# The list schedule of layer 0: a group's operations up to the end of LSTM 0 rank with the group in front of it

## The chip, the cores and the metric

The kernel runs on one core of a Trainium2 chip. The core has five engines with an instruction queue each: PE (matrix products, with weight loads shown as PEld), DVE (vector), ACT (activations and copies), POOL (a second elementwise engine) and SP, which here only issues DMAs. The metric is the device time of the whole program in microseconds (us); lower is better.

## The reference

The input is x, 128 graphs of 64 nodes with 256 features, and one 64 x 64 adjacency matrix. Four layers follow each other, each of the form x = x + layer(relu(layernorm(x))). Only layer 0 is touched by the change:

```python
h = relu(adj @ (h @ Wg0 + bg0))            # twice, with Wg0 and Wg1, per graph
h = relu(adj @ (h @ Wg1 + bg1))
for p in 1..4:                             # four LSTMs of window p
    wins = h[:, :nw*p].reshape(B*nw, p, 256)
    h[:, p-1::p] = lstm_last(Wih[p-1], Whh[p-1], bias, wins)
x = x + h
```

The LSTM of window 1 (here called LSTM 0) has a single step from a zero state, so it needs only the gates i, g and o, no recurrent product, and it overwrites every node. LSTM 1, 2 and 3 have 2, 3 and 4 steps. Layers 1 to 3 are a graph convolution with attention and a feed-forward part, a graph attention layer, and a spectral layer that needs the eigenvectors of a 64 x 64 matrix. That eigendecomposition is computed in the kernel too.

## The kernel before

The 128 graphs are packed in pairs into 64 token tiles of 128 rows. Layer 0 works on groups of GT = 8 tiles, so it has NG = 8 groups; layers 1 to 3 work on 16 groups of HT = 4 tiles.

No instruction is issued where it is written. Every call on an engine goes to a recorder (`Plan.record`), and at the end a list scheduler (`Plan.schedule`, lines 227 to 326) sets the order on each engine from a table of estimated costs, picks the buffers from the pools, and `Plan.issue` emits the whole program; this is why line 344 is the line of every instruction in the profile. The scheduler repeats: for each engine, among the operations whose inputs are done and whose buffers can be had, take the one that can start now with the lowest rank; of the engines, take the one that starts first.

Four things set that choice:

- The window (line 968): while group g is the oldest unfinished one, only groups g and g + 1 of layer 0 may be scheduled. When the last operation of group g has been placed, group g + 2 is admitted. Loads of its input may go one group earlier. This moment is called a boundary below: at boundary k (1 to 7), group k - 1 ends with its transposes and its residual add, and group k + 1 begins with its layernorm statistics (for boundary 7 there is no such group). While group 7 is the oldest, groups of the later layers are admitted.
- The rank (line 328): for layer 0 it is the group's number, less `op.lead`, then `-op.lead`, then the place in the program. An operation recorded with lead 1 thus ranks with the group in front of it, and ahead of that group's own operations.
- The pools: 12 buffers `big` of 128 x 1024, 10 buffers `mids` of 128 x 512, 8 PSUM banks. A group that isn't the oldest must leave some free for the oldest (line 971).
- The eigendecomposition runs beside layer 0 as a group of its own (its tiles are in `arena`). It is a long chain of small DVE operations; it goes last on DVE and ACT and first on PE.

One group of layer 0 (`layer0`, from line 1309) is, in the order of the program:

1. The lead part: statistics of 8 tiles (`ln_stats`: 16 DVE operations, then four small POOL operations for each half of the tiles), 8 ACT operations for normalisation and relu, and for each half a product with adj (`mix`, 32 matmuls of 64 x 64), ACT copies, 8 matmuls with `Wg[0]`, a DVE maximum, a second `mix` and DVE adds; then 8 matmuls of 128 x 512 with `Wg[1]`, each pair followed by a DVE maximum and a POOL add into `hT`.
2. LSTM 0 (`lstm_step` with p = 0): 24 matmuls of 128 x 512 with `Wih[0]`, 12 ACT activations of gates and 4 of tanh, 8 DVE products. It reads and overwrites `hT`, and is the first to use the buffer `cs`.
3. LSTM 1: step 0 is `lstm_step`, 12 matmuls of 128 x 512 with `Wih[1]`. Step 1 is `lstm_fast`, which makes each gate from seven products (Strassen's form) on half-size blocks: 56 matmuls of 128 x 256 with `Wih[1]`, `Whh[1]` and sums of their blocks (`sums`). It needs differences of blocks of the inputs, made on POOL from `hT` and on DVE from `hs` (`pieces`, four operations each).
4. LSTM 2 (in the same manner, 128 x 336 and 128 x 168), and LSTM 3 (plain steps of 128 x 256).
5. The end: 16 transposes of `hT` by PE, four DVE adds into x, and two DMAs to the scratch tensor `put`.

The lines that the change touches are line 1311, which sets the lead to 1 before the statistics, and line 1352, which sets it to 0:

```python
g = min(max(op.group - op.lead, 0), self.ends)
if op.group < REST:
    return (g, -op.lead, op.index)
```

Of the kernel before, what the change touches and what calls it, by code (L numbers as in the profile page):

```python
# [932 lines left out]
def gnn_kernel(ctx: ExitStack, tc: tile.TileContext, a, out):  # L933
# [47 lines left out]
    plan = Plan(tc, {"PE": nc.tensor, "V": nc.vector, "ACT": nc.scalar, "G": nc.gpsimd, "SP": nc.sync}, pools, late, reserve, window, EIG, REST + NT // HT - 6, slack)  # L981
    PE, V, ACT, G, SP = (plan.proxy(e) for e in ("PE", "V", "ACT", "G", "SP"))

    def bank(name):
        return plan.value("bank")
# [179 lines left out]
    def mix(src, m, nt, nc=2):  # L1165

        ps = [bank("mix") for i in range(2)]
        with plan.burst():  # L1170
            for c in range(nc):
                for t in range(nt):
                    for i, r in ((0, 0), (0, 1), (1, 0), (1, 1)):
                        PE.matmul(ps[i][half(r), bat(c * nt + t)], src(t, c)[half(i), half(r)], m(t)[half(i), half(i)], start=True, stop=True)
        return [p[:, :nc * nt * N].rearrange("p (c t n) -> p c t n", c=nc, t=nt) for p in ps]
# [5 lines left out]
    def fm():  # L1181

        return plan.value("big")[:, :2 * HT * P].rearrange("p (c n) -> p c n", c=2)

    def mid():
        return plan.value("mid")

    def transposes(srcs):

        pt = bank("tr")  # L1190
        for i, s in enumerate(srcs):
            PE.transpose(pt[:, i * P:(i + 1) * P], s, ident)
        return pt

    def ln_stats(src, n=HT):

        s = plan.value("stat")
        st = s[:, :6 * n].rearrange("p (t k) -> p t k", k=6)
        mv = s[:, 6 * n:8 * n].rearrange("p (t k) -> p t k", k=2)
        rs = s[:, 8 * n:10 * n].rearrange("p (k t) -> p k t", k=2)  # L1200
        for t in range(n):
            V.bn_stats(st[:, t, :], src[:, t, :])
            V.bn_aggr(mv[:, t, :], st[:, t, :])
        G.tensor_scalar(rs[:, 0, :], mv[:, :, 1], 1e-5, None, op0=ALU.add)
        G.tensor_tensor(rs[:, 0, :], rs[:, 0, :], mhalf[:, :n], op=ALU.pow)
        G.tensor_tensor(rs[:, 1, :], mv[:, :, 0], rs[:, 0, :], op=ALU.mult)
        G.tensor_scalar(rs[:, 1, :], rs[:, 1, :], -1.0, None, op0=ALU.mult)
        return lambda t: rs[:, 0, t:t + 1], lambda t: rs[:, 1, t:t + 1]
# [4 lines left out]
    def lstm_step(p, s, xs, hs, cs, ncol, dsts):  # L1213

        res = {}
        for m in range(2):
            sg = {}
            for nm, q, fn in GATES:
                if s == 0 and nm == "f":
                    continue  # L1220
                col = (q if p > 0 or q == 0 else q - 1) * D + m * P
                ps = bank("gate")[:, :ncol]
                for c in range(2):
                    PE.matmul(ps, Wih[p][:, c, col:col + P], xs(c), start=c == 0, stop=s == 0 and c == 1)
                if s:
                    for c in range(2):
                        PE.matmul(ps, Whh[p][:, c, col:col + P], hs[:, c, :ncol], start=False, stop=c == 1)
                sg[nm] = mid()[:, :ncol]
                ACT.activation(sg[nm], ps, fn, bias=bl[:, p, q * 2 + m:q * 2 + m + 1])
            if s:  # L1230
                V.tensor_mul(sg["i"], sg["i"], sg["g"])
                V.tensor_mul(cs[:, m, :ncol], cs[:, m, :ncol], sg["f"])
                V.tensor_add(cs[:, m, :ncol], cs[:, m, :ncol], sg["i"])
            else:
                V.tensor_mul(cs[:, m, :ncol], sg["i"], sg["g"])
            ACT.activation(sg["g"], cs[:, m, :ncol], AF.Tanh)
            res[m] = (sg["o"], sg["g"])
        for m in range(2):
            o, th = res[m]
            dst = dsts(m)  # L1240
            if len(dst.shape) == 4:
                o, th = (t.rearrange("p (b w t) -> p b w t", b=2, t=GT) for t in (o, th))
            V.tensor_mul(dst, o, th)
# [65 lines left out]
    def layer0(fetched):  # L1309
        x = fetched()  # L1310
        plan.lead = 1
        nl = 2 if plan.group == 0 else HT
        norms = [ln_stats(x[t // HT][:, t % HT:t % HT + nl, :], nl) for t in range(0, GT, nl)]
        ayT = [fm() for hf in range(2)]
        for t0 in range(0, GT, nl):
            sc, bi = norms[t0 // nl]
            two = lambda t: t.rearrange("p (t f) -> p t f", t=2)
            h, ah, y = ([], [], [])
            for j in range(0, nl, 2):
                h.append(two(mid()))  # L1320
                for t in (j, j + 1):
                    ACT.activation(h[-1][:, t - j, :], x[(t0 + t) // HT][:, (t0 + t) % HT, :], AF.Relu, scale=sc(t), bias=bi(t))
            ps = mix(lambda t, c: h[t // 2][:, t % 2, tok(c)], lambda t: adjTb, nl)
            for j in range(0, nl, 2):
                ah.append(mid().rearrange("p (c t) -> p c t", c=2))
                for i in range(2):
                    ACT.copy(ah[-1].rearrange("p c (t b n) -> p c t b n", t=2, b=2)[:, :, :, i, :], ps[i][:, :, j:j + 2, :])
            for j in range(0, nl, 2):
                yp = bank("y")
                for t in range(2):  # L1330
                    for c in range(2):
                        PE.matmul(yp[:, t * D:(t + 1) * D], ah[j // 2][:, c, tok(t)], Wg[0][:, c, :], start=c == 0, stop=c == 1)
                y.append(two(mid()))
                V.tensor_tensor(y[-1], two(yp), vec(nB0, 2), op=ALU.max)
            ps = mix(lambda t, c: y[t // 2][:, t % 2, tok(c)], lambda t: adjTb, nl)
            part = ayT[t0 // HT][:, :, t0 % HT * P:(t0 % HT + nl) * P].rearrange("p c (t b n) -> p c t b n", t=nl, b=2)
            for i in range(2):
                for c in range(2):
                    V.tensor_tensor(part[:, c, :, i, :], ps[i][:, c], vec(C0T[:, c, half(i)], nl), op=ALU.add)

        hT = [plan.value("big")[:, :P * GT] for m in range(2)]
        for hf in range(2):
            ts = slice(hf * GT // 2, (hf + 1) * GT // 2)
            for m in range(2):
                ps = bank("hT")
                for c in range(2):
                    PE.matmul(ps, Wg[1][:, c, tok(m)], ayT[hf][:, c, :], start=c == 0, stop=c == 1)
                dst = hT[m].rearrange("p (n t) -> p n t", t=GT)[:, :, ts]
                b1 = [B1T[:, i, m, :].unsqueeze(2).to_broadcast([P, P, GT // 2]) for i in range(2)]
                V.tensor_tensor(dst, ps.rearrange("p (t n) -> p n t", n=P), b1[0], op=ALU.max)  # L1350
                G.tensor_tensor(dst, dst, b1[1], op=ALU.add)
        plan.lead = 0
        cs, hs = fm(), fm()
        for hf in range(2):
            cols = slice(hf * 512, (hf + 1) * 512)
            lstm_step(0, 0, lambda c: hT[c][:, cols], None, cs, 512, lambda c: hT[c][:, cols])
        for p in range(1, 4):
            k = p + 1
            nw = N // k
            if p == 3:  # L1360
                last = plan.ops[-1]
            for s in range(k):
                def win(c):
                    return hT[c].rearrange("p (b n t) -> p b n t", b=2, t=GT)[:, :, s:s + (nw - 1) * k + 1:k, :]
                ncol = 2 * GT * nw
                dst = win if s == p else lambda c: hs[:, c, :ncol]
                if s and p in (1, 2):
                    w = ncol // 2
                    lstm_fast(p, lambda c, n: win(c)[:, n], lambda c, n: hs[:, c, n * w:(n + 1) * w], cs, w, dst)
                else:  # L1370
                    lstm_step(p, s, win, hs, cs, ncol, dst)

        plan.behind = last
        x = fetched()
        plan.behind = None
        for t0 in range(0, GT, 2):
            pt = transposes([hT[c].rearrange("p (n t) -> p n t", t=GT)[:, :, t0 + t] for t in range(2) for c in range(2)])
            xt = flat(x[t0 // HT][:, t0 % HT:t0 % HT + 2, :])
            V.tensor_add(xt, xt, pt)
        return x  # L1380
# [293 lines left out]
```

## Time and profile before

| | us |
|---|---|
| median of 3 runs (2164.06 to 2165.33) | 2164.6 |
| the profiled execution: its own time | 2165.9 |
| the profiled execution: span from first to last instruction | 2164.1 |
| PE idle in the span (2164.1 less 2112.6 busy) | 51.5 |
| granted PE clock, mean | 0.996 |

The trace divides the span in four. Up to 50 us the first inputs and weights arrive. From there to about 1220 us the groups of layer 0 follow each other, one boundary about every 165 us. From boundary 7 at about 1220 us to 1370 us, group 7 is alone with the end of the eigendecomposition. From 1370 us on, layers 1 to 3 run. Idle time of PE is read from the table of windows (a window's length less PE's busy time), and its cause from the timeline, where the bracket behind an entry names the idle time ahead of it and the engine whose result ended it.

### The profile page before, as it was taken

The numbers are of one execution on the slowest core, as the hardware profiler recorded it, in microseconds if no ns is written. First come the engines' busy times: TensorE is split into PE (matmuls) and PEld (weight loads), VectorE is DVE, ScalarE is ACT, GpSimd is POOL, SyncE is SP. The second block draws the span as 40 slices with busy tenths as digits, with TensorE's granted clock in tenths as the row PEclk, the third lists the DMA queues.
The fourth block names the chain that finished last, engine by engine and source line by source line (L and its number), as shares of the span: only waits on it lengthen the run. The fifth ranks groups of instructions, "written<-read, shape, count | busy, mean of one in ns | idle before, by whom it ended". The sixth has DMA issues, their size and how long they took to land.

```text
span 2164.1 us, 45598 instructions
## 1 busy us (share of the span) xinstructions
PE 2112.6 (98%) x16580; PEld 1630.7 (75%) x16580; DVE 1800.3 (83%) x7402; ACT 1079.8 (50%) x2331; POOL 653.1 (30%) x968
## 2 busy tenths in 40 slices
PE   8999999999999999999999999999999999999997
PEld 6688688688678678678778688766777767776776
DVE  5888788889899999899989887568878868885797
ACT  3354354354354354345345345456566655645673
POOL 7221211210200110110110113654456745554353
PEclk9999999999999999999999999999999999999999
DMA  5000100100100100100000213000010000000001
GB/s 205 2 3 22 41 3 22 40 1 21 40 1 20 40 1 20 40 1 21 26 1 23 69 40 97 21 1 2 21 41 21 21 22 21 12 11 11 1 2 60
DMA packets 44866, 57.67 MB, mean 27 GB/s; under 512 B 8928, under 2 KB 38496, under 8 KB 44640
## 3 DMA queue, kind: packets, MB, share of 16 engines
q1 hardware_dynamic: 43536, 53.71, 7.6%
q8 instruction: 130, 2.13, 0.4%
q10 hardware_dynamic: 1104, 1.05, 0.2%
q14 instruction: 96, 0.79, 0.1%
HBM read 37.53 MB, written 16.78 MB: 25 GB/s over the span
## 4 chain that ended last, share of the span: by engine, by line
PE 83%; DVE 11%; POOL 2%; ACT 1%; DMA 1%; issue 1%; SPq 0%; DVEq 0%; ACTq 0%
PE bank L344 83%; DVE arena L344 3%; DVE big L344 3%; DVE stat L344 2%; DVE mids L344 1%; DVE sums L344 1%; POOL stat L344 1%; POOL sums L344 1%; DMA Wih<-in_WihT_dram 1%; ACT mids L344 0%; ACT arena L344 0%; DMA Whh<-in_L_b_dram 0%; DMA big<-put 0%; ACT big L344 0%; SPq L344 0%
## 5 line engine op out<-in xcount | busy, mean ns | idle before, releaser
L344 PE MATMUL bank<-big,Wih 128*128 128x256 f32 (+3 forms) x2400 | 748.2, 435 | 18.7 <-DVE arena L344 9.3
L344 PEld LDWEIGHTS bank<-big,Wih 128*128 128x128 f32 x2400 | 439.9, 190 | 205.0 <-issue 114.4
L344 ACT ACTIVATE mids<-bank,bl 128x256 f32<-128x256 f32 (+3 forms) x528 | 275.4, 528 | 407.3 <-PE bank L344 403.5
L344 PE MATMUL bank<-big,Whh 128*128 128x256 f32 (+2 forms) x1624 | 431.0, 368 | 3.5 <-DVE big L344 3.5
L344 DVE TENSOR_TENSOR arena<-arena 64x21 f32<-64x21 f32 (+5 forms) x2255 | 372.9, 196 | 35.8 <-POOL arena L344 8.2
L344 PEld LDWEIGHTS bank<-big,Whh 128*128 128x128 f32 x1624 | 294.3, 190 | 42.5 <-issue 10.1
L344 PE MATMUL bank<-big,sums 128*128 128x168 f32 (+2 forms) x1728 | 268.8, 307 | 0.0
L344 PEld LDWEIGHTS bank<-big,sums 128*128 128x128 f32 (+1 forms) x1728 | 225.4, 178 | 16.0 <-issue 3.9
L344 POOL TENSOR_SCALAR stat<-stat 128x4 f32<-128x4 f32 (+1 forms) x228 | 67.9, 299 | 485.4 <-DVE stat L344 472.5
L344 ACT COPY mids<-bank 128x168 f32<-128x168 f32 (+2 forms) x393 | 132.1, 357 | 138.1 <-PE bank L344 135.1
L344 DVE TENSOR_TENSOR big<-mids 128x512 f32<-128x512 f32 (+2 forms) x256 | 142.8, 565 | 31.3 <-ACT mids L344 28.6
L344 ACT ACTIVATE mids<-mids,bl 128x336 f32<-128x336 f32 (+2 forms) x192 | 102.4, 540 | 71.4 <-DVE mids L344 67.6
L344 DVE TENSOR_TENSOR mids<-bank,mids 128x168 f32<-128x168 f32 (+2 forms) x307 | 112.9, 372 | 25.8 <-PE bank L344 22.3
L344 DVE SCALAR_TENSOR_TENSOR arena<-arena 64x1 f32<-64x1 f32 (+15 forms) x565 | 120.9, 237 | 7.5 <-POOL arena L344 3.9
L344 POOL TENSOR_TENSOR big<-big 128x168 f32<-128x168 f32 (+1 forms) x24 | 16.8, 712 | 359.9 <-DVE arena L344 132.2
L344 POOL TENSOR_TENSOR stat<-stat,mhalf 128x4 f32<-128x4 f32 (+1 forms) x114 | 122.1, 1072 | 5.7
L344 ACT ACTIVATE mids<-big 128x256 f32<-128x256 f32 (+2 forms) x176 | 89.4, 509 | 67.7 <-DVE big L344 48.8
L344 PE MATMUL bank<-Wih,big 128*128 128x256 f32 (+1 forms) x512 | 111.7, 358 | 0.2 <-ACT big L344 0.2
L344 DVE TENSOR_SCALAR arena<-arena 64x1 f32<-64x1 f32 (+9 forms) x537 | 104.8, 202 | 8.4 <-POOL arena L344 0.8
L344 DVE TENSOR_TENSOR big<-big,mids 128x256 f32<-128x256 f32 (+2 forms) x200 | 99.3, 498 | 11.1 <-ACT mids L344 10.2
L344 PEld LDWEIGHTS bank<-Wih,big 128*128 128x128 f32 x512 | 87.7, 190 | 15.4 <-issue 4.5
L344 ACT COPY big<-bank 128x512 f32<-128x512 f32 x108 | 59.9, 587 | 55.9 <-PE bank L344 50.8
(357 smaller groups left out, 3568.0 us busy)
## 6 DMA issues: line engine op xcount, KB each, us to landing
big<-in_x_dram SPq DMA_DIRECT2D x30, 512.0 KB, 5.2
put<-big SPq DMA_DIRECT2D x16, 512.0 KB, 3.0
Wih<-in_WihT_dram SPq DMA_DIRECT2D x3, 1024.0 KB, 11.8
Whh<-in_WhhT_dram SPq DMA_DIRECT2D x3, 1024.0 KB, 13.8
big<-put SPq DMA_DIRECT2D x6, 512.0 KB, 5.8
arena<-put SPq DMA_DIRECT2D x6, 512.0 KB, 6.6
out_dram<-big SPq DMA_DIRECT2D x12, 256.0 KB, 2.3
out_dram<-arena SPq DMA_DIRECT2D x12, 256.0 KB, 2.3
```

The lines of the kernel that those rows point to most:

```text
L344: getattr(self.engines[op.eng], name)(*map(real, args), **{k: real(a) for k, a in kw.items()})
```

## The change

The line that sets the lead back to 0 moves from ahead of LSTM 0 to behind it. All operations of LSTM 0 of a group now have lead 1: they rank with the group in front, ahead of that group's own operations. No operation is added or removed, and no size changes.

```diff
-        plan.lead = 0
         cs, hs = fm(), fm()
         for hf in range(2):
             cols = slice(hf * 512, (hf + 1) * 512)
             lstm_step(0, 0, lambda c: hT[c][:, cols], None, cs, 512, lambda c: hT[c][:, cols])
+        plan.lead = 0
         for p in range(1, 4):
```

## The prediction, made before the changed kernel had run

> **What bounds the kernel now.** I read the page's busy shares first, then the table of windows around the boundaries, then the timeline of one boundary, engine by engine.
>
> ```profile
> PE 2112.6 (98%) x16580; PEld 1630.7 (75%) x16580; DVE 1800.3 (83%) x7402; ACT 1079.8 (50%) x2331; POOL 653.1 (30%) x968
> ```
>
> PE is busy for 98% of the span, and the change gives it the same matmuls. So all that can be won or lost is PE's idle time, 51.5 us in all. By windows of 50 us it divides into 7.1 before 50 us, 11.2 from 50 to 1200, 12.1 from 1200 to 1400, 8.8 from 1400 to 2100 and 12.3 behind that. Within layer 0 it is nearly all at the seven boundaries (first column: the window; then its length; then PE busy):
>
> ```profile
> 223.00:256.00 33.00, 31.77 (x349) 19.56 (x348) 26.60 (x119) 13.63 (x35) 10.84 (x20) 1.00 0.20 66
> 391.00:424.00 33.00, 31.59 (x349) 19.65 (x348) 28.36 (x124) 13.26 (x35) 10.30 (x20) 1.00 0.20 66
> 557.00:593.00 36.00, 34.80 (x356) 21.09 (x355) 31.04 (x139) 12.77 (x27) 10.39 (x15) 1.00 0.18 60
> 720.00:756.00 36.00, 34.28 (x360) 22.16 (x360) 32.79 (x105) 12.55 (x27) 8.96 (x14) 1.00 0.18 60
> 884.00:921.00 37.00, 34.07 (x352) 20.92 (x351) 31.54 (x141) 12.75 (x27) 9.44 (x14) 0.95 0.17 58
> 1050.00:1086.00 36.00, 33.81 (x353) 20.57 (x352) 30.95 (x139) 12.95 (x27) 10.41 (x15) 1.00 0.11 38
> 1216.00:1240.00 24.00, 20.36 (x65) 11.32 (x64) 21.69 (x82) 8.32 (x14) 10.71 (x20) 0.96 0.41 142
> ```
>
> Length less busy gives 1.23, 1.41, 1.20, 1.72, 2.93, 2.19 and 3.64 us: 14.3 us together. The timeline of PE at boundary 3 shows what a boundary is:
>
> ```profile
> 557.72 0.60 PE L344 MATMUL bank<-ident,big 128*128 128x128 f32 x4
> 558.16 1.88 PE L344 MATMUL bank<-big,Wih 128*128 128x512 f32 x4
> 559.88 1.50 PE L344 MATMUL bank<-ident,big 128*128 128x128 f32 x12
> 561.22 5.32 PE L344 MATMUL bank<-big,Wih 128*128 128x512 f32 x12
> 567.73 3.67 PE L344 MATMUL bank<-big,Wih 128*128 128x512 f32 x8 [1.20 <-DVE arena L344]
> 571.34 1.16 PE L344 MATMUL bank<-adjTb,mids 64*64 64x64 f32 x64
> 572.43 1.98 PE L344 MATMUL bank<-big,Wih 128*128 128x512 f32 x4
> ```
>
> The old group's 16 transposes (128x128) come in two parts: four read half of `hT` that is done, twelve wait for its last DVE product. Between and behind them lie 8 matmuls of LSTM 0 of the next group (128x512; each leaves two records). Then PE waits 1.20 us, because LSTM 1 needs LSTM 0's result, whose DVE products stand behind the new group's 16 statistics operations (563.10 to 566.3). Then come 4 matmuls of LSTM 1, the first `mix` at 571.34, and 3 more of LSTM 1 between the mixes. Everything in 128x512 with `Wih` is filler: work that PE has while the new group's statistics (DVE), scales (POOL, 565.18 to about 567.4), normalisation (ACT, from 567.71) and mixes run one after another.
>
> [...] at 567.73 PE waits for a DVE product that had to let 3.2 us of statistics pass, though other matmuls were to come. [...] Here the repeated gap is a data wait; whether buffers add to it, no run shows yet.
>
> **The change part by part.** (a) It removes and adds nothing. It moves LSTM 0 of each group (24 matmuls at 0.865 us, from 6 matmuls in 5.2 us; 16 ACT operations of 0.62 to 0.69 us; 8 DVE products of 0.68 us; no DMA, so SP's queue issues the same loads and stores; no POOL operation of its own, though POOL's block differences for LSTM 1 follow it earlier) from the slot "when nothing of the old group is ready" to "as soon as `hT` is there".
>
> (b) The order of the two programs on PE shows this. At boundary 3, eigendecomposition apart (L0, L1: 128x512; F: 128x256 of LSTM 1's fast step):
>
> ```
> before: tr4 L0x2 tr12 L0x6 L1x4 mix L1x2 Wg0x8 mix L1x1 mix Wg0x8 Wg1x2 mix Wg1x6 L1x5 L0x5 ...
> after:  tr4 tr12 Fx19 mix Fx1 mix Wg0x11 mix Wg0x5 Wg1x2 mix Wg1x6 Fx3 L0x24 ...
> ```
>
> Before, 15 fillers of 0.865 us (13.0 us) stand between the transposes and the last Wg1 product. After, LSTM 0 is long done and LSTM 1's step 0 has been used up as filler inside the old group's LSTM 2 and 3; what is left are 20 halves of 0.43 us, or 8.6 us. Counted in whole matmuls, the fillers at boundaries 1 to 6 go from 16, 15, 15, 13, 13, 14 to 10, 10, 10, 9, 10, 15.5. Inside the old group the slots are filled as before, by LSTM 1 in place of LSTM 0.
>
> (c) Boundary 3 worked out, from L3's end at 557.72. The twelve transposes wait for the DVE product, which three block differences of 0.42 us each now precede: about 559.55 in place of 559.88, of which 1.4 us is idle since no filler stands there. Adds and statistics then end about 0.15 us sooner than before. ACT's normalisation starts about 567.4, since LSTM 0's tanh is no longer ahead of it (before: 567.71). The first mix can start at 569.6; PE has run 19 x 0.43 = 8.2 us since 560.9, so it waits 0.5. The second mix needs eight normalisations of 0.51 us: 571.7, a wait of 0.65. Then DVE has three large eigendecomposition operations ahead of the maxima (the reduction alone takes 3.08 us elsewhere in the trace), and the adds: about 0.5, 0.45 and 0.8 before `Wg1`. That is 4.3 us of waits; by difference (the end of Wg1 at 590.7 against 592.75 before, 4.3 us less filler, 1.2 us waited before) it is 3.5. I take 3.9. A second path: before, 13 fillers go with a mean wait of 2.3 us, 15 or 16 with 1.3, so 0.4 us for each missing matmul; at 10 fillers this gives 3.5, and 4.9 if each costs its full 0.865. Both agree.
>
> (d) Boundaries 1 and 5 have the same order: 3.9 each. At 2 and 4 one LSTM 1 matmul stands between the transposes (0.55 in place of 1.4), but the last product of LSTM 1's step 0 stands behind the adds, and three of its four block differences behind the statistics: I take 4.6 and 4.9. At 6 there is filler for all but the transposes: 1.5. At 7 nothing of layer 0 enters; before, 1.16 and 2.48 us were lost as step 0 of LSTM 1 led into its fast step, which now was done before: 0.5. Sum 23.2, less 14.3: +8.9 us.
>
> (e) LSTM 0 as a block of 24 on PE (20.8 us) needs 16 ACT operations (about 10.5 us) and 8 DVE products (5.4 us): hidden behind PE. Its first two matmuls need only the first half of `hT` and so cover POOL's last add (1.11 us, ending 2.1 us behind Wg1's end at boundary 3). Were this cover gone, it is the 1.80 us that PE waited for POOL at 35.62: up to 6 x 1.8 = 11 us; I take nothing.
>
> (f) Layers 1 to 3 are ordered anew from 1371 us on. The last 1064 of 8578 matmuls (about the last 200 us) stand in the same order, so the 12.3 us at the end stay. The 8.8 us between may change by 4 either way; I take nothing. The eigendecomposition ends slightly earlier against LSTM 3 in the new order, so it is not late.
>
> **The rivals.** (A) As above: fillers are spent inside the group and lacking at the boundary. 2164.6 + 8.9 = 2173.5; on the profiled execution 2165.9 + 8.9 = 2174.8. The run shown is 1.3 above the median; I forecast the median. Own range 2168 to 2179.
> (B) No change: the statistics chain is freed of LSTM 0's 0.69 us ACT and 0.68 us DVE operations and is 1.5 us shorter at five boundaries than I took; 8.9 - 7.5 gives about 2166.
> (C) Faster: the wait for LSTM 0's last product, which is all of the 14.3 us, vanishes, and fast products cover the rest. Left would be the transposes: 4 x 1.4 + 2 x 0.55 = 6.7; 2164.6 - 14.3 + 6.7 = 2157. For it: that wait stands in every bracket. Against it: 8.6 us of filler for a chain for which 13.0 were not enough. It decides if the first mix is ready 8.2 us behind the transposes and nothing waits after it.
> (D) Worse: the fast step also stalls inside, [...] and its banks are freed by DVE behind statistics and eigendecomposition. Two more us at each of five boundaries: 2183. For it: the DVE order; against it: the order already puts the mix where the fast step would block.
> That the change does nothing is excluded by the two orders.
>
> **How the numbers follow.** Chances: A 0.53, B 0.17, C 0.16, D 0.14. The time is A's, 2173.5. The range 2161 to 2184 takes in B and D and most of (f)'s spread, and leaves out most of C. What can be told from no change is about 0.2%, 4.3 us: slower is A and D, nearly all: 0.66; within is B: 0.18; faster is C: 0.16.
>
> **What would show it.** Right: idle PE of 3.5 to 5 us at boundaries 1 to 5, a bracket at the twelve transposes naming DVE, one at the first mix naming ACT, none behind LSTM 0. Wrong: boundary windows with under 2 us idle (B or C), brackets inside LSTM 1's products (D), or a change of the idle time behind 1371 us of more than 4 us, which would mean that the later layers decide.

## The result, and the profile after

The changed kernel takes 2173.6 us (median of 5 runs, 2172.35 to 2175.2), the kernel before 2164.9 on the same chip: a ratio of 1.0036, 95% interval 1.0025 to 1.0048. It is slower by 8.7 us. The profiled execution is the median run; its span is 2171.8 us, 7.7 above the span of before.

The line of busy time of the changed kernel (busy us, share of the span, instructions):

```profile
PE 2117.2 (97%) x16580; PEld 1631.6 (75%) x16580; DVE 1795.9 (83%) x7402; ACT 1055.9 (49%) x2315; POOL 652.9 (30%) x968
```

The instructions of PE are the same, yet it is "busy" 4.6 us longer. So only 3.1 of the 7.7 us show as idle time, and idle time is not the whole of what PE loses. Two things hide in busy time: waits of some 0.1 to 0.3 us between matmuls, as the ends in the records are modelled, and stretches at half clock. I therefore measure by starts as well: the interval from the start of one PE record to the next, less the 0.43, 0.22, 0.14 or 0.11 us that a record of this shape (512, 256, 168, 128 columns; the other shapes in the same way) takes where the records stand close. I call this sum "waits". Some 0.9 us of it at each of boundaries 1 to 6 is the passing into and out of the four mixes, before and after alike.

The windows of the changed kernel's boundaries 1 to 7 (length, then PE busy; the first figure behind POOL's count is PE's clock):

```profile
245.00:279.00 34.00, 31.86 (x372) 23.96 (x371) 27.34 (x110) 11.22 (x34) 9.17 (x17) 1.00 0.19 64
414.00:448.00 34.00, 32.80 (x370) 23.71 (x370) 26.19 (x112) 11.14 (x33) 10.53 (x18) 1.00 0.19 64
582.00:616.00 34.00, 31.63 (x368) 23.68 (x367) 29.57 (x81) 10.48 (x26) 12.28 (x14) 1.00 0.19 63
746.00:781.00 35.00, 31.67 (x359) 23.15 (x358) 28.68 (x134) 9.93 (x25) 9.46 (x14) 0.95 0.19 62
914.00:946.00 32.00, 30.64 (x366) 23.19 (x366) 27.96 (x127) 10.36 (x26) 9.99 (x14) 1.00 0.20 67
1078.00:1114.00 36.00, 34.83 (x383) 26.68 (x384) 32.37 (x119) 11.60 (x29) 9.71 (x14) 1.00 0.11 38
1240.00:1266.00 26.00, 25.59 (x127) 22.39 (x126) 22.84 (x96) 10.11 (x24) 7.50 (x15) 1.00 0.46 152
```

Length less busy is 2.14, 1.20, 2.37, 3.33, 1.36, 1.17 and 0.41 us: 12.0 together, where before had 14.3. The boundaries as a whole did not get worse. The timeline of PE at boundary 3 shows which waits are there (the bracket: idle time ahead of the entry, and the engine whose result ended it):

```profile
582.75 0.61 PE L344 MATMUL bank<-ident,big 128*128 128x128 f32 x4
584.65 1.60 PE L344 MATMUL bank<-ident,big 128*128 128x128 f32 x12 [1.29 <-DVE big L344]
...
595.48 0.70 PE L344 MATMUL bank<-big,sums 128*128 128x256 f32 x2
596.81 2.29 PE L344 MATMUL bank<-adjTb,mids 64*64 64x64 f32 x64 [0.64 <-ACT mids L344]
599.08 5.02 PE L344 MATMUL bank<-Wg,mids 128*128 128x256 f32 x22
```

The twelve transposes wait for the last DVE product without a filler, a mix waits for ACT, and behind it there is nothing. The loss is elsewhere. In the changed kernel PE stops at the hand-over from LSTM 2 to LSTM 3 of group 0:

```profile
192.62 0.45 PE L344 MATMUL bank<-big,sums 128*128 128x168 f32 x2
194.14 0.49 PE L344 MATMUL bank<-arena 128*128 128x128 f32 x2 [1.07 <-DVE arena L344]
195.05 0.55 PE L344 MATMUL bank<-big,Wih 128*128 128x168 f32 x2 [0.43 <-DVE mids L344]
195.44 0.45 PE L344 MATMUL bank<-big,Whh 128*128 128x168 f32 x2
197.05 3.29 PE L344 MATMUL bank<-big,Wih 128*128 128x256 f32 x14 [1.16 <-DVE big L344]
```

At the same place in the kernel before, two 128x512 filler matmuls (two records each) stand in the gap, one in the first line and one in the fourth. The view merges records of one tile, so the fourth line holds two records of 128x512 and two of 128x168:

```profile
170.54 1.02 PE L344 MATMUL bank<-big,Wih 128*128 128x512 f32 x2
171.40 0.45 PE L344 MATMUL bank<-big,sums 128*128 128x168 f32 x2
171.68 0.45 PE L344 MATMUL bank<-big,Whh 128*128 128x168 f32 x2
171.97 1.31 PE L344 MATMUL bank<-big,Wih 128*128 128x512 f32 x4
173.11 0.45 PE L344 MATMUL bank<-big,Whh 128*128 128x168 f32 x2
173.40 3.62 PE L344 MATMUL bank<-big,Wih 128*128 128x256 f32 x16
```

In the changed kernel the last filler of that phase starts at 176.6 us, and with it filler of this kind is used up: LSTM 0 and step 0 of LSTM 1 of groups 0 and 1 have 144 records, of which 51 start before 82.8 us and 93 from there to 176.6. LSTM 1's fast step would come next, but it needs step 0's last two products. The last gate for these ends on ACT at 177.96 us; the products start on DVE at 245.92 us and directly behind it, at the boundary, though operations of the eigendecomposition, which rank behind them on DVE, run in between. They are the first to write the buffer `hs` of the new group, so by the scheduler's rules a buffer of the pool `big` is the likely thing they wait for. No run gives that pool more room: whether PE lacks matmuls here or the matmuls lack a buffer was not tested.

The sum of waits by stage, in us, for the two kernels and the experiments told below ("group phases": from the end of `Wg1` of one boundary to the transposes of the next; the last two columns are times, not waits):

| | phase of group 0 | phases 1 to 6 | boundaries 1 to 6 | boundary 7 | group 7 alone | layer 1 starts at | layers 1 to 3 take |
|---|---|---|---|---|---|---|---|
| before | 14.4 | 0.2 | 19.1 | 5.7 | 9.1 | 1363.0 | 801.1 |
| the change | 20.4 | 1.2 | 22.7 | 0.5 | 9.9 | 1369.1 | 802.7 |
| PE alone | 21.0 | 1.2 | 22.5 | 0.0 | 9.5 | 1368.7 | 802.8 |
| ACT and DVE alone | 15.3 | -0.5 | 11.9 | 1.9 | 13.5 | 1356.1 | 809.1 |
| ACT and DVE, two steps | 16.1 | -0.5 | 12.4 | 2.7 | 9.4 | 1354.4 | 810.2 |
| the same, later order kept | 15.4 | -0.5 | 12.4 | 1.8 | 9.6 | 1353.1 | 807.8 |
| group 7 only | 14.6 | 6.2 | 19.1 | 0.3 | 9.5 | 1364.2 | 806.7 |
| group 1 only | 19.2 | 0.1 | 22.0 | 6.8 | 11.8 | 1374.3 | 806.0 |
| half of LSTM 0 | 17.9 | 3.8 | 13.6 | 3.0 | 10.1 | 1362.8 | 802.3 |
| half, from group 4 on | 14.2 | 5.8 | 12.4 | 6.4 | 10.1 | 1363.3 | 804.7 |

So the 7.7 us of the change are: group 0's phase +5.9, the other phases +1.0, boundaries 1 to 6 +3.5, boundary 7 -5.1, group 7 alone +0.8, layers 1 to 3 +1.6 (rounded). Not all of the first is the change's: up to 43.5 us PE has the same order in both kernels, and there, at the first record that differs, the change is already 1.0 us behind (44.57 us against 43.54). Boundary 7 gains more than its idle time, because of PE's clock. Four windows of 2 us at boundary 5 of the kernel before (the figure before the last two is the clock):

```profile
894.00:896.00 2.00, 0.57 (x2) 0.36 (x3) 2.00 (x7) 1.22 (x3) 1.76 (x4) 1.00 1.04 351
896.00:898.00 2.00, 2.00 (x5) 0.88 (x4) 1.76 (x13) 1.49 (x4) 1.75 (x5) 0.67 0.15 52
898.00:900.00 2.00, 2.00 (x3) 0.79 (x3) 1.93 (x5) 0.28 (x1) 1.92 (x3) 0.50 0.00 0
900.00:902.00 2.00, 2.00 (x67) 1.20 (x66) 1.24 (x7) 1.96 (x5) 0.77 (x2) 0.98 0.00 0
```

Behind the wait of 2.93 us PE runs at half clock: 2 x 0.33 + 2 x 0.50 + 2 x 0.02 = 1.7 us are lost while it counts as busy. The same 1.7 follow the wait of 2.48 us at boundary 7 of before. The change has neither, but one at boundary 4, and 5.1 us of half clock in the first 25 us where before had 3.4.

### The profile page after: what moved, and what is told of

It reads as the page before. It is cut to its first block, busy times and chain, and to the rows that moved or that the text cites. A ratio compares the mean times of both kernels' runs of the same rounds, so it can differ in the third digit from the quotient of the medians.

```text
span 2171.8 us, 45615 instructions
## 1 busy us (share of the span) xinstructions
PE 2117.2 (97%) x16580; PEld 1631.6 (75%) x16580; DVE 1795.9 (83%) x7402; ACT 1055.9 (49%) x2315; POOL 652.9 (30%) x968
## 5 line engine op out<-in xcount | busy, mean ns | idle before, releaser
L344 PE MATMUL bank<-big,Wih 128*128 128x256 f32 (+3 forms) x2352 | 719.7, 430 | 4.7 <-DVE mids L344 2.5
L344 PE MATMUL bank<-big,Whh 128*128 128x256 f32 (+3 forms) x1704 | 440.7, 364 | 3.7 <-DVE big L344 3.7
L344 PEld LDWEIGHTS bank<-big,Whh 128*128 128x128 f32 (+1 forms) x1704 | 297.7, 188 | 44.5 <-issue 10.8
L344 ACT COPY mids<-bank 128x168 f32<-128x168 f32 (+2 forms) x378 | 122.4, 349 | 136.0 <-PE bank L344 132.1
L344 ACT ACTIVATE mids<-mids,bl 128x336 f32<-128x336 f32 (+3 forms) x192 | 102.1, 541 | 137.8 <-DVE mids L344 135.8
L344 POOL TENSOR_TENSOR big<-big 128x168 f32<-128x168 f32 (+1 forms) x24 | 15.4, 648 | 466.6 <-ACT mids L344 313.3
L344 DVE SCALAR_TENSOR_TENSOR arena<-arena 64x1 f32<-64x1 f32 (+16 forms) x567 | 124.0, 241 | 9.1 <-POOL arena L344 4.8
L344 DVE TENSOR_TENSOR mids<-bank,mids 128x168 f32<-128x168 f32 (+2 forms) x296 | 104.9, 361 | 14.3 <-PE bank L344 7.2
L344 DVE TENSOR_SCALAR arena<-arena 64x1 f32<-64x1 f32 (+8 forms) x538 | 104.5, 201 | 7.6 <-POOL arena L344 0.2
L344 DVE TENSOR_TENSOR big<-big,mids 128x256 f32<-128x256 f32 (+2 forms) x196 | 97.0, 495 | 11.9 <-ACT mids L344 11.1
L344 PE MATMUL bank<-Wih,big 128*128 128x256 f32 (+1 forms) x424 | 98.6, 373 | 0.0
L344 PEld LDWEIGHTS bank<-Wih,big 128*128 128x128 f32 x424 | 75.9, 190 | 13.8 <-issue 4.5
L344 POOL TENSOR_TENSOR arena<-arena 64x1 f32<-64x1 f32 x66 | 40.4, 612 | 124.8 <-ACT arena L344 99.0
```

The lines of the kernel that those rows point to most:

```text
L344: getattr(self.engines[op.eng], name)(*map(real, args), **{k: real(a) for k, a in kw.items()})
```

## The experiments

The theory at first was the prediction's own, that filler lacks at the boundaries; its rivals there are named in each expectation. Experiment 1 showed the loss in another place, and from experiment 5 on "the theory" is this: LSTM 0 and the following step of LSTM 1 are PE's stock of filler. The change uses LSTM 0 as one block and spends LSTM 1's step 0 soon behind it, so the last phases of the old group stand bare, while the boundaries lose something and win something.

**1. The change in group 7 only.**

```diff
+        if not (plan.group == 7):
+            plan.lead = 0
         cs, hs = fm(), fm()
```

> LSTM 0 has lead 1 in group 7 alone; the order of PE is that of the kernel before up to boundary 6. Filler theory: the change costs where filler is spent (boundaries, LSTM phases of the old group) and gains only at boundary 7, where step 0 of LSTM 1 is already done: 5.1 us less waiting in the window of boundary 7, nothing lost at boundary 6, where the first mix has its fillers as before: about 2160 us, ratio 0.9975 to 0.998. Rival, alignment with the eigendecomposition: what was gained at boundary 7 was luck of that one order, so within 1.5 us of before (2163.5 to 2166.5). A new order of layers 1 to 3 can add 2 us either way.

Measured: 2172.59 us (8 runs), ratio 1.0025 (1.0015 to 1.0036). Both missed. Up to boundary 6 each stage's waits repeat those of before within 0.2 us. Boundary 7 loses 5.4 us of waits, as in the change, but group 6's phase, for which neither had a figure, waits 6.1 more, again up to the hand-over to LSTM 3:

```profile
1187.55 0.45 PE L344 MATMUL bank<-big,Wih 128*128 128x168 f32 x2
1187.83 0.45 PE L344 MATMUL bank<-big,Whh 128*128 128x168 f32 x2
1189.86 2.42 PE L344 MATMUL bank<-big,Wih 128*128 128x256 f32 x10 [1.58 <-DVE big L344]
```

And layers 1 to 3, whose program is untouched, take 5.6 us more.

**2 and 3. Without the eigendecomposition.** Two kernels, before and the change, leave the eigendecomposition out (layer 3 gets the identity in place of the eigenvectors). The room of its tiles is kept closed until layer 0 is done; that line of the edit is not shown.

```diff
-    QT, Vc, inner = eig_decomp(plan, room, adj2[:N], adjT2[:N], ident[:N, :N], ident, ones)
+    QT, Vc = room.tile([P, N]), room.tile([P, N])
+    for t in (QT, Vc):
+        V.tensor_copy(t, ident[:, :N])
+    inner = Carver(room.cut(NEIG))
```

> The kernel before without the eigendecomposition (its two results are copies of the unit matrix; its room is kept closed until layer 0 is done). All groups then have the same order on PE. Both theories: waits of 1 to 2.5 us at each of boundaries 1 to 6 and none inside the groups; total below before by the waits that the eigendecomposition caused, 2150 to 2163 us.

> The changed kernel without the eigendecomposition, to be compared with e2. Filler theory: at each of boundaries 1 to 6 the waits are 1 to 2.5 us longer than in e2, at boundary 7 they are 4 to 5 us shorter: 2 to 9 us slower than e2. Rival, alignment with the eigendecomposition: the waits at boundaries 1 to 6 are as in e2 within 0.5 us each, so e3 is up to 5 us faster than e2.

Measured: 2137.69 and 2139.13 us (4 runs each), 1.4 apart; the second scatters from 2136.8 to 2146.0, so the sign of this is not sure. The time of 2 lies 12 us below its range, which was reckoned from waits alone: PE's busy time, too, falls by 17.6 us (2095.0 in place of 2112.6). Its waits at the boundaries came as expected. Both times that were expected of 3 are missed. By stage (profiles) the change does the same as in the whole kernel, but smaller where DVE was crowded: group 0's phase +4.4, boundaries 1 to 6 +2.3 together (each 0.3 to 0.5, from 1.5 to 2.0 before), boundary 7 -3.3, group 7 alone -2.6 (1.7 of it half clock), layers 1 to 3 +1.5. So my filler theory's size for the boundaries (1 to 2.5 each) is wrong, and the rival's (within 0.5 each) is right within 0.02; the loss in group 0's phase is there without any eigendecomposition.

**4. Only the first half of LSTM 0** (its first 512 columns).

```diff
             lstm_step(0, 0, lambda c: hT[c][:, cols], None, cs, 512, lambda c: hT[c][:, cols])
-        plan.lead = 0
+            plan.lead = 0
```

> Only the first half of LSTM 0 (12 of 24 matmuls) has lead 1. Filler theory: the second half stays as filler for the old group's LSTM phases, and step 0 of LSTM 1, unused, stands at the boundary: 18 to 20 matmuls' worth of filler between the transposes and the first Wg1 product in place of 10: waits at boundaries 1 to 5 of at most 2.5 us each (changed kernel: 2.6 to 6.7), total 2160 to 2166 us. Rival: each moved product costs alike, so half of the loss remains: about 2169 us.

Measured: 2165.80 us (12 runs), ratio 0.9996 (0.9988 to 1.0005): no difference from before, inside the theory's range and under the rival's 2169. Boundaries 1 to 5 wait 2.6, 1.6, 1.9, 1.8 and 2.0 us, about as the theory had it, but phases 0 to 2 wait 5.8 more and layers 1 to 3 take 1.2 more, so that nearly all is given back.

**5. The change in group 1 only** (the edit of 1, with `plan.group == 1`).

> LSTM 0 ranks with the group in front in group 1 alone. Theory (inside the old group the filler runs out: LSTM 0 goes as one block, LSTM 1's step 0 is spent directly behind it, and LSTM 2's hand-over to LSTM 3 stands bare): group 0's phase up to its transposes waits 4 to 6 us more than before, boundary 1 +1.5, all later stages of layer 0 within 1.5 together; time +4 to +8 on before. Rival (the prediction's own: the filler lacks at the boundary only): group 0's phase within 1 us of before, boundary 1 +2.5 or more; time +2 to +4.

Measured: 2181.57 us (4 runs), ratio 1.0075 (1.0061 to 1.0089). The place of the loss is shown: group 0's phase +4.8 and boundary 1 +1.5, as in the theory and against the rival. But the time is 16 us up, not 4 to 8. At boundary 4, where the rules are those of before, the scheduler now put two filler records between the last transposes and the first mix in place of fourteen:

```profile
731.32 1.50 PE L344 MATMUL bank<-ident,big 128*128 128x128 f32 x12
732.65 1.02 PE L344 MATMUL bank<-big,Wih 128*128 128x512 f32 x2
740.63 2.82 PE L344 MATMUL bank<-adjTb,mids 64*64 64x64 f32 x64 [6.95 <-ACT mids L344]
743.38 3.77 PE L344 MATMUL bank<-big,Wih 128*128 128x512 f32 x4
```

The wait of 6.95 us is followed by half clock (0.50) up to 747 us: this boundary costs 8.1 us more than before. Why the scheduler left the filler behind the mix there is not settled. Layers 1 to 3 again take 4.9 more.

**6 and 7. Filler held back.** Both are the change with half of LSTM 1's step 0 (6 of 12 matmuls, with their gates) made to depend on a point in the old group: the end of LSTM 2's middle step (6), or of LSTM 3's third step (7).

```diff
+            if p == 1 and s == 0 and m == 1:
+                plan.behind = tails.get(plan.group - 1)
...
+                if p == 2 and s == 2:
+                    tails[plan.group] = plan.ops[-1]
```

> The change, and half of LSTM 1's step 0 of the group behind (6 of its 12 matmuls) may not start until the old group has done LSTM 2's middle step. Theory (filler spent too early): group 0's phase falls from +5.9 us on before to +2.5 or less, since six matmuls of 0.43 us with their eleven and more of LSTM 1's fast step come where it was bare; boundaries as in the change or 1 us lower each. Rival (not the filler, but LSTM 0's ACT and DVE operations in front of LSTM 2's own): group 0's phase stays at +5 or more, as these operations are where they were.

> The change, and the same half of LSTM 1's step 0 held until the old group has done LSTM 3's third step, so that it is left for the boundary. Theory (one stock of filler, spent either inside or at the boundary): boundaries 1 to 6 together fall by 3 us or more from the change's 22.6, and group 0's phase stays at +5 or more; time 2170 to 2175. Rival (the boundaries of the change are set by the transposes' wait and by DVE, not by filler): boundaries within 2 us of the change's sum.

Measured: 2197.85 and 2211.07 us (4 runs each), ratios 1.0147 and 1.0214. The time of 7 misses by far; for 6 none had been given. What they show is the place: in 6 eight filler records run from 187 to 193 us and the hand-over of group 0 has no wait any more, but a wait of 0.96 and one of 0.38 us stand at 172 and 174 us, where the filler was taken from; the phase still waits 4.6 us more than before (the theory had at most 2.5, the rival 5 or more). In 7 both places are bare (+8.0). Phases 1 to 6 then wait 15.0 and about 28 us in place of 1.2, and boundaries 1 to 6 do not fall but rise, to 32.1 and 28.5. So in these two runs filler held back by a fixed rule moved the wait along, and cost more than filler spent too early. Neither the theory's nor the rival's figure for the boundaries in 7 holds.

**8. Half of LSTM 0, from group 4 on** (the edit of 4, and `plan.lead = 0` ahead of it for groups below 4).

> Half of LSTM 0 (its first half of columns) ranks with the group in front, in groups 4 to 7 alone; groups 1 to 3 as before. Theory (with half of LSTM 0 kept as filler the boundaries 4, 5 and 7 lose their waits, and where nothing was to be won the order of before costs nothing): boundaries 4, 5 and 7 together fall by 5 to 8 us from before, group phases within 1, the later layers +0 to +2; time 2159 to 2163, faster than both. Rival (those gains come from the place at which the eigendecomposition stood in the run with half everywhere): the sum over boundaries falls by less than 3, time 2164 to 2168.

Measured: 2168.94 us (21 runs), ratio 1.0015 (1.0008 to 1.0021). Boundary 5 falls by 3.9, boundary 4 by 1.2 and 6 by 1.6; boundary 7 rises by 0.8, phases 3, 5 and 6 wait 5.6 more, layers 1 to 3 take 3.6 more. The theory's time, its sum for boundaries 4, 5 and 7 (-4.3 in place of -5 to -8) and its claim on the phases are missed, and so are the rival's time and sum.

**9 and 10. The two sides of the change.** In 9 only LSTM 0's ACT and DVE operations rank with the group in front, in 10 only its matmuls. The edit of 9 is shown (a third line sets the lead to 0 behind LSTM 0); in 10 the two values are exchanged.

```diff
                 ps = bank("gate")[:, :ncol]
+                plan.lead = 0
                 for c in range(2):
                     PE.matmul(ps, Wih[p][:, c, col:col + P], xs(c), start=c == 0, stop=s == 0 and c == 1)
...
+                plan.lead = int(p == 0)
                 sg[nm] = mid()[:, :ncol]
```

> The change for ACT and DVE alone: the gates, tanh and products of LSTM 0 rank with the group in front, its matmuls keep their own rank. Theory (the change has two parts: on PE it takes filler out of the boundary and out of the old group's last phases, and that costs; on DVE it sets LSTM 0's last product ahead of the new group's statistics, and that gains): PE's order stays that of before but for a few fillers, group 0's phase stays within 1.5 us of before, and boundaries 1 to 7 together fall by 4 to 10 us from before's 24.8; the half-clock stretches behind boundaries 5 and 7 go. Time 2156 to 2163. Rival (the wait behind LSTM 0 is not set by the order on DVE, but by the last gate's own length from PE over ACT to DVE): boundaries within 2 us of before, time 2163 to 2168.

> The change for PE alone: LSTM 0's matmuls rank with the group in front, its ACT and DVE operations do not. PE's order of layer 0's matmuls is the change's. Theory: group 0's phase +4 to +6 on before, boundaries 1 to 6 together as in the change within 2, time 2172 to 2177. Rival (what hurts the old group's phase is LSTM 0's ACT and DVE work in front of LSTM 2's own): group 0's phase within 2 us of before.

Measured: 10 takes 2172.71 us (5 runs), ratio 1.0033 (1.0021 to 1.0045), and is the change, stage by stage: group 0's phase +6.6 (the theory had 4 to 6, the rival under 2), boundaries 1 to 6 22.5. So what the change does, it does by the matmuls. 9 is something else. Boundaries 1 to 7 fall by 11.0 us, group 0's phase is within 0.9 us of before, and layer 1 starts 6.9 us earlier than before. PE at boundary 5 of before, and then of 9:

```profile
888.91 3.60 PE L344 MATMUL bank<-big,Wih 128*128 128x512 f32 x8
895.43 5.37 PE L344 MATMUL bank<-big,Wih 128*128 128x512 f32 x8 [2.93 <-DVE arena L344]
900.73 1.16 PE L344 MATMUL bank<-adjTb,mids 64*64 64x64 f32 x64
```

```profile
886.59 4.46 PE L344 MATMUL bank<-big,Wih 128*128 128x512 f32 x10
891.57 7.10 PE L344 MATMUL bank<-big,Wih 128*128 128x512 f32 x16 [0.53 <-ACT mids L344]
898.61 1.16 PE L344 MATMUL bank<-adjTb,mids 64*64 64x64 f32 x64
```

and DVE at the same place, before:

```profile
893.50 0.39 DVE L344 BATCH_NORM_STATS2 stat<-big 128x6 f32<-128x256 f32 x1
893.81 0.29 DVE L344 BATCH_NORM_AGGREGATE stat<-stat 128x2 f32<-128x6 f32 x2
894.02 1.26 DVE L344 TENSOR_TENSOR big<-mids 128x512 f32<-128x512 f32 x2
```

and in 9:

```profile
889.84 0.39 DVE L344 BATCH_NORM_STATS2 stat<-big 128x6 f32<-128x256 f32 x1
890.15 1.27 DVE L344 TENSOR_TENSOR big<-mids 128x512 f32<-128x512 f32 x2
891.35 0.23 DVE L344 BATCH_NORM_AGGREGATE stat<-stat 128x2 f32<-128x6 f32 x2
```

Two of LSTM 0's products now stand among the statistics and not behind all sixteen; PE waits 0.53 in place of 2.93 us, and the half clock behind it is gone (clock 1.00 from 891 to 905 us). Yet 9 takes 2168.87 us (21 runs), ratio 1.0016 (1.0009 to 1.0022), where before has 2165.17, in place of 2156 to 2163: in the profiled execution (2166.99 us, 1.9 under the median) layers 1 to 3 take 8.0 us more than before and give all back. The rival's figures are missed as well.

**11. ACT and DVE alone, in step 0 of LSTM 1 as well** (`int(p < 2 and s == 0)`).

> As the run for ACT and DVE alone, and the same for step 0 of LSTM 1 (its matmuls keep their rank too). Theory (what is won is the product's place ahead of the statistics, so LSTM 1's product gains in the same way where the fast step follows at boundaries 1, 5 and 7): boundary 7 falls by 2 to 4 us below before, total 1 to 3 us below the run with LSTM 0 alone. Rival (whatever is moved at one boundary comes back at another through the place of the eigendecomposition): total within 3 us of the run with LSTM 0 alone, on either side, with single boundaries off by more than 2.

Measured: 2166.89 us (13 runs), ratio 1.0007 (0.9999 to 1.0016), 2.0 below experiment 9; boundary 7 falls by 3.0 from before, but rises by 0.7 against 9. The theory's two figures are met, but not by its reason: against 9 boundary 5 also rises, by 1.5, and the gain lies in group 7's stretch alone (-4.1). The rival's total is met as well, its single boundaries off by more than 2 are not. Layer 1 starts 8.6 us earlier than before, and layers 1 to 3 take 9.1 more.

**12. The same, with the order of layers 1 to 3 kept.** The scheduler runs twice: once with the ranks of before, to note the order of the later layers on each engine, and again with the ranks of 11, where a later operation may be issued only if it is next in that order.

```diff
+                    if self.follow and op.group >= REST and op.group != self.aside and self.follow[e][0] is not op:
+                        continue
```

> As the run for ACT and DVE of two steps, but the operations of layers 1 to 3 are issued on each engine in the order that the kernel before gives them; layer 0 keeps the order of the two-steps run. That run had layer 0 done 8.6 us earlier than before and lost 9.1 us in layers 1 to 3 (810.2 against 801.1). Theory (the loss is the new order that the list scheduler finds for layers 1 to 3 when anything ahead of them moves): layers 1 to 3 take 801 to 804 us, time 2156 to 2161, faster than both kernels. Rival (the loss is the time at which layer 0 and the eigendecomposition end and what they leave behind, not the order): layers 1 to 3 take 808 us or more, time 2164 to 2168.

Measured: 2164.32 us (13 runs), ratio 0.9991 (0.9983 to 0.9999). It is the only version whose interval lies below before, if only just; the medians are 1.7 us apart, and by the two ratios it is 0.4% below the change. The theory's time is missed, the rival's (2164 to 2168) is met. Layers 1 to 3 take 807.8 us, 6.8 of it lost to half clock, where before loses 1.7 and experiment 11 1.7. Less this loss the three are 801.0, 799.4 and 808.5: keeping the order wins back 7.5 of the 9.1 us. But where layer 1 now begins, 9.9 us earlier, PE waits for its inputs:

```profile
1355.76 3.03 PE L362 MATMUL bank<-lapb,arena 64*64 64x64 f32 x192
1362.14 2.45 PE L362 MATMUL bank<-lapb,arena 64*64 64x64 f32 x64 [3.35 <-ACT big L362]
1366.72 0.48 PE L362 MATMUL bank<-lapb,arena 64*64 64x64 f32 x4 [2.13 <-ACT big L362]
1367.69 1.87 PE L362 MATMUL bank<-lapb,arena 64*64 64x64 f32 x58 [0.49 <-ACT big L362]
```

and 5.1 of the half clock lies at 1361 to 1372 us. So both sides of the question hold in part, though neither figure for layers 1 to 3 (801 to 804, 808 or more) was met. The profiled execution is the fastest of the 13; the stages of the others were not read.

## Why the prediction was right, and where it was not

The time came out within 0.1 us of the forecast (2173.56 against 2173.5), but by terms that made up for each other, so that its closeness is luck. The mechanism (filler spent too early) is the right one, the place was not.

- Step (a): right. Nothing added or removed; the 4.6 us by which PE's busy time rose is waiting that the records show as busy.
- Step (b), first half: right, PE's order at the boundaries is the one predicted. Its last sentence, "Inside the old group the slots are filled as before, by LSTM 1 in place of LSTM 0", is the step that failed. Group 0's phase lost 5.9 us and group 5's 1.3. 3.1 of the 5.9 are the three waits at the hand-over of LSTM 2, with the passing into and out of them (1.23, 0.59 and 1.32 by starts); 1.7 are half clock in the first 25 us, a loss that is 5.1 in eight of the experiments' profiles, 3.4 in three and 1.7 in one, with and without the change, so that I don't ascribe it to the change; at 43.5 us, where the orders part, 1.0 of it is left. The rest of the 5.9 was not traced. Experiments 1, 3, 5 and 10 show the loss where a group's LSTM 0 is drawn ahead as a block and its LSTM 1 follows: 6.1, 4.4, 4.8 and 6.6 in the old group's phase (in 10, too, 1.0 of this is there before the orders part). Groups 1 to 4 show none: in group 1's phase the last six filler records start from 360.0 to 365.2 us, at the hand-over itself. Why it lasts until the hand-over there, and not in group 0's phase, is left open.
- Step (c): the transposes' wait of 1.4 came as 1.29, the second mix's 0.65 as 0.64. The first mix's 0.5 and the three waits ahead of `Wg1` (0.5, 0.45, 0.8) did not come: 1.9 us of idle time where I took 3.9 in all (2.37 with three gaps of 0.15 inside the second mix). The rule of 0.4 us for each missing filler, drawn from before's boundaries, does not hold: experiment 9 shows that the largest of these waits was set by the place of LSTM 0's product on DVE.
- Step (d): idle time at the seven boundaries 12.0 in place of 23.2. At boundary 7, 0.41 for 0.5: right; but the gain there was 5.1 and not 3.1, as the half clock behind the old wait went too: in before, the clock is 0.75, 0.50 and 0.90 in the three windows of 2 us from 1237 us on, behind the wait of 2.48 us, a loss of 1.7 us. The prediction had no term for it.
- Step (e): right. No wait behind LSTM 0's block, none for POOL behind `Wg1` at boundary 3.
- Step (f): +1.6 us within the 4 that were allowed. As a bound it was luck: the same layers took 1.2 to 9.1 us more than before in experiments 1, 4, 5, 8, 9, 11 and 12.
- The rivals: C's mechanism is real. The wait behind LSTM 0 is gone at boundaries 5 and 7, which with its half clock wait 8.2 us less in all, by starts; it was outweighed by what C did not price. D (stalls inside) was put in the fast step behind the boundary; the stalls came at the end of LSTM 2.
- What was to be seen: the brackets came as named (DVE at the transposes, ACT at a mix, none behind LSTM 0), but idle times of 2.1, 1.2, 2.4, 3.3 and 1.4 us at boundaries 1 to 5 are below the 3.5 to 5 that A asked for, and those at 2 and 5 are under the 2 us that it named as a sign of B or C. By that mark the forecast's reason was wrong though its number was right.

Of the 8.7 us, experiments 2 and 3 leave 1.4, within their scatter, without the eigendecomposition. The rest is how the change falls in with that chain and with PE's clock; which part each has was not separated.

## What to carry to other kernels

In a list schedule an operation that is "moved ahead" is also filler taken from somewhere: ask of each phase, not only of the one in view, what PE has left when its chain is bare, and whether the freed filler may be held without forbidding its use. Move the short operations that others wait for (here LSTM 0's products on DVE) and leave the long ones that fill: that won 6.9 us in layer 0, where moving both lost 6.1, though the program as a whole was not faster for it. Ask also whether filler that seems to be lacking waits for a buffer. And read the gain at the end of the stage as well as at the end of the program, since whatever is scheduled behind can give it back.

## What the runs showed of the hardware and the schedule that was not expected

- In before, the waits of 2.93 us (boundary 5) and 2.48 us (boundary 7) were each followed by 3.4 us at half clock, a loss of 1.7 us that counts as busy. The length of a wait alone does not decide it: waits of 2.69 us (experiment 4, 1237 us), 2.75 us (experiment 10, 1377 us) and 2.56 us (experiment 11, 1482 us) were not followed by half clock, nor was the single wait of 1.58 us (before, 730 us). In the clock records of the fourteen traces every stretch at half clock that the trace's end doesn't cut lasts 3.41, 6.83 or 10.24 us, a loss of 1.7, 3.4 or 5.1 us.
- Three short waits within 14 us at boundary 4 of the change were followed by such a stretch (clock 0.57 from 762 to 766 us):

```profile
748.63 1.60 PE L344 MATMUL bank<-ident,big 128*128 128x128 f32 x12 [0.72 <-DVE big L344]
752.40 0.70 PE L344 MATMUL bank<-big,Whh 128*128 128x256 f32 x2 [0.88 <-DVE big L344]
761.61 1.53 PE L344 MATMUL bank<-adjTb,mids 64*64 64x64 f32 x60 [1.57 <-ACT mids L344]
```

  No single long wait stands there, in the change (1.57 us is the longest) as in experiment 10, which has the same stretch at 762 to 766 us; that the short waits brought it about is inferred from their place.
- One wait of 6.95 us was followed by 6.4 us of work at half clock, 3.2 us lost (experiment 5).
- Where the order of instructions is the same, the trace repeats: the waits of groups 1 to 5 in experiment 1 agree with before within 0.02 us per stage.
- The order of untouched layers is worth as much as the change: 7.5 us between experiments 11 and 12, by profiles less half clock.
